# One-core GNN stack: bits and f columns by transfers, norm statistics on GpSimd, wider softmax products

## The chip, the cores and the metric

The kernel runs on one core of one Trainium2 chip. The metric is the device time of one execution in microseconds. The time before the change is the median of three runs.

## The reference, cut to what matters

Each of 64 independent graphs has 256 nodes with 256 features, and goes through four layers. Each layer's result is added to its input and normalised over the features.

```python
# layer 0: transformer layer with 8 heads of 32, masked by the symmetric adjacency
allowed = (adj > 0) | (swapaxes(adj, 1, 2) > 0) | eye
attn = softmax(where(allowed, (q * scale) @ k.T, -inf))          # per head
x = layernorm(x + (attn @ v) @ Wo.T + bo) ; x = layernorm(x + relu(x @ W1.T + b1) @ W2.T + b2)
# layers 1 and 2: graph attention
h = x @ W ; f = h @ a[0] ; g = h @ a[1]
e = leaky_relu(f[:, None] + g[None, :], 0.2), masked by adj > 0
out = softmax(e) @ h            # (+ bias in layer 1, elu in layer 2)
# layer 3: two relational convolutions with elu, on masks adj == 1
# after each layer: x = _layernorm(x + layer(x))
def _layernorm(x, eps=1e-5):
    m = mean(x) ; v = var(x)
    return (x - m) / sqrt(v + eps)
```

## The kernel before

A graph's work is written as a list of operations with estimated costs and lags, their reads and writes, and rings of buffers. A planner inside the kernel (`Plan.schedule`) runs through all 64 graphs' operations once, when the kernel is built, and fixes the order of the instructions on each engine; several graphs are under way at once, and on the chip every engine goes through its list strictly in that order. `pe(...)`, `dve(...)` and `act(...)` put an operation on TensorE, VectorE and ScalarE; `op("POOL", ...)` and `op("SP", ...)` on GpSimd and SyncE. The marks "uses" and "waits" tell the planner to keep GpSimd's norm operations apart from VectorE operations with two SBUF operands; they are no waits on the chip.

The helpers that the change touches or that the prediction speaks of (bodies cut where nothing changes):

```python
def add_later(xt, yt, reads):
    op("POOL", 0.6, lambda: nc.gpsimd.dma_start(xt(), yt(), accum_op=ALU.add), [xt, *reads], [xt], lag=3.0)

def bounced(xt):            # a transposed copy: blocks on VectorE, then rows through DRAM
    dve(0.63, ... nc.vector.transpose(turned..., xt...), [xt], [turned], "uses")
    for a in range(4):
        op("SP", 0.5, lambda a=a: nc.sync.dma_start(rows()...[:, :, a, :], turned()[32 * a : 32 * a + 32]...), [turned], [(rows, a)], lag=SENT)
    op("SP", 0.5, lambda: nc.sync.dma_start(xT()..., rows()...), [rows], [xT], lag=BACK)

def layer_norm(y):
    mv, stat = new("mv", [P, NB, 2]), new("st", [P, NB, 6])
    rstd = new("rstd", [P, 2, NB])
    def stats():
        for i in range(NB):
            nc.vector.bn_stats(stat()[:, i, :], y()[:, i, :])
        for i in range(NB):
            nc.vector.bn_aggr(mv()[:, i, :], stat()[:, i, :])
    def root():
        nc.gpsimd.tensor_scalar(rstd()[:, 0, :], mv()[:, :, 1], 1.0, EPS, op0=ALU.mult, op1=ALU.add)
        nc.gpsimd.tensor_tensor(rstd()[:, 0, :], rstd()[:, 0, :], neghalf[:, 0:NB], op=ALU.pow)
        nc.gpsimd.tensor_tensor(rstd()[:, 1, :], mv()[:, :, 0], rstd()[:, 0, :], op=ALU.mult)
        nc.gpsimd.tensor_scalar(rstd()[:, 1, :], rstd()[:, 1, :], -1.0, 1.0, op0=ALU.mult, op1=ALU.mult)
    def apply():
        for i in range(NB):
            nc.scalar.activation(y()[:, i, :], y()[:, i, :], AF.Identity, bias=rstd()[:, 1, i : i + 1],
                                 scale=rstd()[:, 0, i : i + 1])
    dve(0.88, stats, [y], [mv, stat])
    op("POOL", 1.6, root, [mv], [rstd], port="waits", lag=0.4)
    act(1.0, apply, [y, rstd], [y])

def masks(adj):
    bits, am, gm = tok("bits", BF16), tok("am", BF16), tok("gm", BF16)
    pt = new("bank", [P, NB, N], BF16)
    dve(0.33, lambda: nc.vector.tensor_scalar(bits(), adj(), 0.0, None, op0=ALU.is_gt), [adj], [bits], "uses")
    def issue():
        for i in range(NB):
            for j in range(NB):
                nc.tensor.transpose(pt()[:, i, j * P : (j + 1) * P], bits()[:, j, i * P : (i + 1) * P], ident_b)
    pe("full", 0.22, issue, [bits], [pt], [am, gm])
    dve(0.33, lambda: nc.vector.tensor_scalar(gm(), pt(), BIG, NO_EDGE, op0=ALU.mult, op1=ALU.add), [pt], [gm])
    dve(0.33, lambda: nc.vector.tensor_tensor(am(), pt(), bits(), op=ALU.max), [pt, bits], [am])
    ...                      # the diagonal of am is set

def attention(xT, am):
    ...                      # projections; two halves kt of the keys
        pe("row", 0.97, scores, [qk], s, [p[kt, r] for r in range(4)])
        for r in range(4):
            pr, k = p[kt, r], 8 * g + 4 * kt + r
            act(0.58, lambda pr=pr, k=k, sr=s[r]: nc.scalar.activation(
                pr(), sr(), AF.Exp, accum_out=seen_sum[:, k : k + 1]), [s[r]], [pr])
            dve(0.60, lambda pr=pr, kt=kt: nc.vector.tensor_tensor(
                pr(), pr(), am()[:, kt, None, :].to_broadcast([P, KB, N]), op=ALU.mult), [pr, am], [pr], "uses")
    both = [new("both", [P, KB, N]) for r in range(4)]
    for r in range(4):
        dve(0.60, lambda r=r: nc.vector.tensor_tensor(both[r](), p[0, r](), p[1, r](), op=ALU.add),
            [p[0, r], p[1, r]], [both[r]], "uses")
    ...                      # products with v, reciprocals

def feed_forward(x1, xt):
    add_row_later(xt, ln2b)
    x1T = transposed(x1)
    with_row(x1, ln1g, ALU.mult)
    with_row(x1, b2, ALU.add)
    ...

def gat(xt, layer, gm, seen, bias, finish):
    xT, xT_at = bounced(xt)
    ...                      # h = x W, with the columns f and g beside it
    pf = new("bank", [P, N])
    def spread():
        for i in range(NB):
            nc.tensor.transpose(pf()[:, i * P : (i + 1) * P],
                                h()[:, i, F_COL : F_COL + 1].to_broadcast([P, P]), ident)
    pe("full", 0.22, spread, [(h, 0), (h, 1)], [pf], [e])
    for i in range(NB):
        dve(0.40, lambda i=i: nc.vector.scalar_tensor_tensor(e()[:, i, :], pf(), h()[:, i, G_COL : G_COL + 1],
                                                             gm()[:, i, :], op0=ALU.add, op1=ALU.min),
            [pf, (h, i), gm], [(e, i)])
    dve(0.60, lambda: nc.vector.scalar_tensor_tensor(e(), e(), SLOPE, e(), op0=ALU.mult, op1=ALU.max), [e], [e],
        "uses")
    act(0.52, lambda: nc.scalar.activation(e(), e(), AF.Exp), [e], [e])
    ...                      # products e h, each row divided by its sum

# one graph
xT = input_transposed()
adj = load("adj", adj_graph[g], I32)
am, gm = masks(adj)
xt = load("x", x_graph[g], F32)
add_row_later(xt, bo, [c_bo])
ctxT = attention(xT, am)
x1 = product_plus(lambda c: ctxT()[:, c, :], [ctxT, c_wo], lambda c: wo[:, c, :], KB, xt)
layer_norm(x1)
xt = feed_forward(x1, load("xr", x_graph[g], F32))
xt = layer1(xt, gm)
xt = layer2(xt, gm)
rel = relation(load("adj", adj_graph[g], I32))
rdeg = new("rdeg", [P, NB])
h = conv(conv(xt, 0, rel, rdeg), 1, rel, rdeg)
add(h, xt)
layer_norm(h)
op("SP", 0.4, lambda: nc.sync.dma_start(out_graph[g], h()), [h], [])
```

## Time and profile before

| | before |
|---|---|
| time, median of 3 | 2897.77 us (2897.14 to 2898.14) |
| span of the profiled execution | 2897.1 us, 50588 instructions |
| TensorE clock granted | 0.991 of full, mean |
| HBM | 157.43 MB read, 83.89 MB written |
| transfers issued by SyncE | 37.7% of 16 DMA engines' span |
| transfers issued by GpSimd | 8.5% |
| `rows<-turned`, `T<-rows`, `blocks<-in_x` | 1024, 256 and 512 transfers |

The profile names engines PE (TensorE matmuls), PEld (its weight loads, which overlap matmuls), DVE (VectorE), ACT (ScalarE), POOL (GpSimd) and SPq (the queue of SyncE, which issues transfers). A group line gives the line of the kernel, the engine, the operation, output and input tiles with their shapes, and the count; then busy us and the mean ns of one; then the idle time of the engine just before instructions of the group, and what ended it. Line numbers can be those of a helper: L657 is the matmul of every product. An f32 matmul appears as two instructions.

The page's chain of work that ended last is TensorE for 82% of the span, with 67% on line L657 alone; VectorE has 10%, ScalarE 3%, transfers 2%.

### The profile page before, as it was taken

The page shows a single profiled execution, that of the slowest core. Times are in us where ns is not written, and L with a number is a line of the kernel's source. Part 1 is how long each engine was busy: PE and PEld are TensorE (multiplying, and loading weights), DVE is VectorE, ACT ScalarE, POOL GpSimd, SP SyncE. Part 2 cuts the span into 40 slices and gives each one's busy share as a digit, 9 for nine tenths or more (in the row PEclk, how much of TensorE's full clock was granted, in tenths as well). Part 3 has the DMA queues.
Part 4 walks back from the last instruction along what each step waited for, and adds up shares of the span by engine and source line. Part 5 has one row for each costly group of instructions (what it writes and reads, how often), then busy time and mean ns, then how long its engine had stood idle before and what let it go on. Part 6 is the DMA issues. An engine that isn't in the chain of part 4 may idle for free.

```text
span 2897.1 us, 50588 instructions
## 1 busy us (share of the span) xinstructions
PE 2805.3 (97%) x16182; PEld 2128.1 (73%) x16182; DVE 2523.0 (87%) x6557; ACT 1540.4 (53%) x3713; POOL 789.1 (27%) x1685
## 2 busy tenths in 40 slices
PE   8999999999999999999999999999999999999975
PEld 6776777777777767777777777777777777777853
DVE  6879899989989898999889898899888998999686
ACT  3555555546455555655555465555555655555343
POOL 2232223222223222222222322232231332222221
PEclk9999999999999999999999999999999999999998
DMA  7454455445444444454444544444444544443342
GB/s 183 81 108 88 99 101 102 89 101 102 95 92 100 87 94 94 98 101 93 104 97 93 98 99 99 100 91 102 86 93 96 109 88 93 105 90 72 67 83 70
DMA packets 844512, 278.32 MB, mean 96 GB/s; under 512 B 692656, under 2 KB 810672, under 8 KB 844240
## 3 DMA queue, kind: packets, MB, share of 16 engines
q1 hardware_dynamic: 808800, 240.27, 37.7%
q0 software_dynamic: 35440, 34.76, 8.5%
q8 instruction: 131, 2.15, 0.3%
q14 instruction: 141, 1.16, 0.1%
HBM read 157.43 MB, written 83.89 MB: 83 GB/s over the span
## 4 chain that ended last, share of the span: by engine, by line
PE 82%; DVE 10%; ACT 3%; DMA 2%; issue 2%; POOL 1%; SPq 1%; DVEq 0%; POOLq 0%; ACTq 0%
PE bank L657 67%; PE bank L919 4%; PE bank L776 3%; PE bank L751 3%; PE bank L771 2%; DMA rows<-turned 2%; DVE p L759 1%; PE bank L618 1%; DVE turned L629 1%; PE bank L839 1%; SPq L633 1%; DVE st L666 1%; DVE o L929 1%; DVE both L763 1%; DVE e L844 1%
## 5 line engine op out<-in xcount | busy, mean ns | idle before, releaser
L671 POOL TENSOR_SCALAR rstd<-mv 128x2 f32<-128x2 f32 x384 | 104.4, 272 | 1869.8 <-DVE mv L668 1496.7
L678 ACT ACTIVATE X<-X,rstd 128x256 f32<-128x256 f32 x640 | 349.8, 597 | 244.7 <-POOL rstd L674 230.1
L657 PE MATMUL bank<-cw,T 128*128 128x512 f32 x1024 | 467.9, 600 | 9.6 <-DMA T<-rows 9.1
L657 PE MATMUL bank<-T,w 128*128 128x256 f32 x2048 | 471.6, 380 | 5.2 <-ACT p L757 2.6
L657 PE MATMUL bank<-w,hid 128*128 128x256 f32 x2048 | 460.1, 380 | 0.0
L657 PEld LDWEIGHTS bank<-w,hid 128*128 128x128 f32 x2048 | 385.9, 190 | 62.7 <-issue 10.4
L657 PEld LDWEIGHTS bank<-T,w 128*128 128x128 f32 x2048 | 382.7, 190 | 64.5 <-issue 6.9
L757 ACT ACTIVATE p<-bank 128x512 f32<-128x512 f32 x512 | 299.9, 598 | 87.8 <-PE bank L751 87.6
L657 PEld LDWEIGHTS bank<-cw,T 128*128 128x128 f32 x1024 | 192.2, 192 | 209.3 <-issue 195.2
L759 DVE TENSOR_TENSOR p<-p,am 128x512 f32<-128x512 f32 x512 | 332.8, 680 | 10.8 <-ACT p L757 10.7
L672 POOL TENSOR_TENSOR rstd<-rstd,neghalf 128x2 f32<-128x2 f32 x384 | 305.7, 796 | 32.1
L809 ACT ACTIVATE hid<-bank,col_b 128x256 f32<-128x256 f32 x512 | 209.4, 474 | 113.8 <-PE bank L657 112.1
L657 PE MATMUL bank<-xT,wqkv 128*128 128x256 f32 x1024 | 251.6, 387 | 13.4 <-DVE xT L650 12.9
L657 PE MATMUL bank<-h,e 128*128 128x259 f32 x1024 | 253.8, 388 | 11.0 <-ACT e L849 9.3
L657 PE MATMUL bank<-gw,T 128*128 128x258 f32 x1024 | 249.1, 384 | 2.1 <-ACT inv L783 1.5
L657 PEld LDWEIGHTS bank<-h,e 128*128 128x128 f32 x1024 | 192.7, 192 | 66.6 <-issue 19.3
L666 DVE BATCH_NORM_STATS2 st<-X 128x6 f32<-128x256 f32 x640 | 237.5, 413 | 1.8
L906 ACT CAST hi<-bank 128x256 fp32r<-128x256 f32 x256 | 94.6, 370 | 263.4 <-PE bank L657 262.6
L657 PEld LDWEIGHTS bank<-xT,wqkv 128*128 128x128 f32 x1024 | 189.7, 192 | 54.0 <-issue 13.5
L780 DVE RECIPROCAL inv<-bank 128x256 f32<-128x256 f32 x128 | 220.0, 1734 | 8.8 <-PE bank L776 8.6
L657 PEld LDWEIGHTS bank<-gw,T 128*128 128x128 f32 x1024 | 191.1, 191 | 36.7 <-issue 5.2
L629 DVE STREAM_TRANSPOSE turned<-X 128x512 f32<-128x512 f32 x192 | 134.9, 703 | 45.0 <-DMA rows<-turned 23.0
(121 smaller groups left out, 4775.4 us busy)
## 6 DMA issues: line engine op xcount, KB each, us to landing
rows<-turned SPq DMA_DIRECT2D x1024, 64.0 KB, 2.2
T<-rows SPq DMA_DIRECT2D x256, 256.0 KB, 2.8
adj<-in_adj_dram SPq DMA_DIRECT2D x128, 256.0 KB, 3.0
blocks<-in_x_dram SPq DMA_DIRECT2D x512, 32.0 KB, 2.3
x<-in_x_dram SPq DMA_DIRECT2D x64, 256.0 KB, 3.0
xr<-in_x_dram SPq DMA_DIRECT2D x64, 256.0 KB, 2.8
xr<-row_ln_b POOLq DMA_DIRECT2D x64, 256.0 KB, 4.4
x<-row_bo POOLq DMA_DIRECT2D x64, 256.0 KB, 4.8
```

What stands on the lines that cost most here:

```text
L629: dve(0.63, lambda: nc.vector.transpose(turned().rearrange("p b q n -> p (b q n)"), xt().rearrange("p i (k b c) -> p b (i k) c", k=KB, b=4 ...
L657: nc.tensor.matmul(dst, lhsT=lhs(c), rhs=rhs(c), start=(c == 0), stop=(c == n - 1))
L666: nc.vector.bn_stats(stat()[:, i, :], y()[:, i, :])
L671: nc.gpsimd.tensor_scalar(rstd()[:, 0, :], mv()[:, :, 1], 1.0, EPS, op0=ALU.mult, op1=ALU.add)
L672: nc.gpsimd.tensor_tensor(rstd()[:, 0, :], rstd()[:, 0, :], neghalf[:, 0:NB], op=ALU.pow)
L678: nc.scalar.activation(y()[:, i, :], y()[:, i, :], AF.Identity, bias=rstd()[:, 1, i : i + 1], scale=rstd()[:, 0, i : i + 1])
L757: act(0.58, lambda pr=pr, k=k, sr=s[r]: nc.scalar.activation(pr(), sr(), AF.Exp, accum_out=seen_sum[:, k : k + 1]), [s[r]], [pr])
L759: dve(0.60, lambda pr=pr, kt=kt: nc.vector.tensor_tensor(pr(), pr(), am()[:, kt, None, :].to_broadcast([P, KB, N]), op=ALU.mult), [pr, am] ...
L780: dve(1.62, lambda hg=hg, pc=pc: nc.vector.reciprocal(inv()[:, hg, :], pc()[:, 1, :]), [pc], [(inv, hg)])
L809: act(0.36, lambda f=f, k=k, ph=ph: nc.scalar.activation(hid()[:, f + k, :], ph()[:, k, :], AF.Relu, bias=b1[:, f + k : f + k + 1]), [ph, ...
L906: act(0.27, lambda i=i, po=po: nc.scalar.copy(hi()[:, i, 0:D], po()[:, D:]), [po], [(hi, i)])
L919: nc.tensor.matmul(pa()[:, 0:n], lhsT=rel()[:, i, j * P : (j + 1) * P], rhs=part()[:, i, 0:n], start=(c == 0), stop=(c == len(terms) - 1))
```

## The change: what it does and what it is for

Seven things change.

1. The adjacency bits (bf16) are transposed by four transposing transfers for each graph (128x128 each, SBUF to SBUF) in place of four TensorE transposes into PSUM. The masks `gm` and `am` are then made from SBUF.
2. The column f, which each partition needs as a row, is spread by transfers in place of two TensorE transposes with a broadcast operand: VectorE turns 32x32 blocks of the column repeated 32 times, two transfers write them as rows to DRAM, and one transfer reads these rows into all 128 partitions. `e` is made from SBUF.
3. The norm's two halves of statistics, which VectorE's `bn_stats` leaves, are joined on GpSimd in place of VectorE's `bn_aggr`; GpSimd then has nine small operations for a norm in place of four.
4. The row b2 is added by an accumulating transfer, in place of VectorE.
5. The last residual is added by an accumulating transfer, except in the last two graphs.
6. The softmax products and sums on VectorE take 1024 elements at a time in place of 512. The buffers double in size and halve in number.
7. The planner is told a spacing of 44 in place of 46 us between graphs.

Its aim is to take work off TensorE and VectorE and give it to the DMA engines and GpSimd.

The diff, with unchanged lines cut and the indentation shortened:

```diff
@@ ... @@
-RINGS = {"x": 3, "adj": 4, "bits": 2, "am": 2, "gm": 6, "T": 4, "qk": 2, "v": 2, "p": 12, "both": 4, "inv": 1, "ctxT": 2, "X": 8,
-         "xr": 1, "hid": 1, "h": 3, "e": 3, "n": 1, "rel": 3, "hi": 2, "lo": 2, "o": 4, "blocks": 1, "turned": 1, "xT": 2}
-DRAM = {"rows": 6}
+RINGS = {"x": 3, "adj": 4, "bits": 2, "am": 2, "gm": 6, "T": 4, "qk": 2, "v": 2, "p": 6, "both": 2, "inv": 1, "ctxT": 2, "X": 8,
+         "xr": 1, "hid": 1, "h": 3, "e": 3, "n": 1, "rel": 3, "hi": 2, "lo": 2, "o": 4, "blocks": 1, "bitsT": 1, "f": 2, "own": 2, "turned": 1, "xT": 2}
+DRAM = {"f_row": 2, "rows": 6}
@@ ... @@
-    PERIOD = 46.0
+    PERIOD = 44.0
@@ ... @@
 def layer_norm(y):
-    mv, stat = new("mv", [P, NB, 2]), new("st", [P, NB, 6])
-    rstd = new("rstd", [P, 2, NB])
+    stat, t, rstd = new("st", [P, NB, 2, 3]), new("mv", [P, NB, 4]), new("rstd", [P, 2, NB])
         for i in range(NB):
-            nc.vector.bn_stats(stat()[:, i, :], y()[:, i, :])
-        for i in range(NB):
-            nc.vector.bn_aggr(mv()[:, i, :], stat()[:, i, :])
+            nc.vector.bn_stats(stat()[:, i].rearrange("p h k -> p (h k)"), y()[:, i, :])
-        nc.gpsimd.tensor_scalar(rstd()[:, 0, :], mv()[:, :, 1], 1.0, EPS, op0=ALU.mult, op1=ALU.add)
-        nc.gpsimd.tensor_tensor(rstd()[:, 0, :], rstd()[:, 0, :], neghalf[:, 0:NB], op=ALU.pow)
-        nc.gpsimd.tensor_tensor(rstd()[:, 1, :], mv()[:, :, 0], rstd()[:, 0, :], op=ALU.mult)
-        nc.gpsimd.tensor_scalar(rstd()[:, 1, :], rstd()[:, 1, :], -1.0, 1.0, op0=ALU.mult, op1=ALU.mult)
+        tensor_tensor, tensor_scalar = nc.gpsimd.tensor_tensor, nc.gpsimd.tensor_scalar
+        m, s, d = t()[:, :, 0], t()[:, :, 1], t()[:, :, 2]
+        scale, shift = rstd()[:, 0, :], rstd()[:, 1, :]
+        tensor_tensor(t()[:, :, 0:2], stat()[:, :, 0, 1:3], stat()[:, :, 1, 1:3], op=ALU.add)
+        tensor_tensor(d, stat()[:, :, 0, 1], stat()[:, :, 1, 1], op=ALU.subtract)
+        tensor_tensor(d, d, d, op=ALU.mult)
+        tensor_scalar(s, s, 4 / D, 4 * EPS, op0=ALU.mult, op1=ALU.add)
+        tensor_tensor(d, d, s, op=ALU.add)
+        tensor_tensor(d, d, neghalf[:, 0:NB], op=ALU.pow)
+        tensor_tensor(shift, m, d, op=ALU.mult)
+        tensor_scalar(shift, shift, -1.0, 1.0, op0=ALU.mult, op1=ALU.mult)
+        tensor_scalar(scale, d, 2.0, 1.0, op0=ALU.mult, op1=ALU.mult)
         for i in range(NB):
-    dve(0.88, stats, [y], [mv, stat])
-    op("POOL", 1.6, root, [mv], [rstd], port="waits", lag=0.4)
+    dve(0.56, stats, [y], [stat])
+    op("POOL", 2.5, root, [stat], [t, rstd], port="waits", lag=0.6)
 def masks(adj):
-    pt = new("bank", [P, NB, N], BF16)
+    pt = tok("bitsT", BF16)
-    def issue():
-        for i in range(NB):
-            for j in range(NB):
-                nc.tensor.transpose(pt()[:, i, j * P : (j + 1) * P], bits()[:, j, i * P : (i + 1) * P], ident_b)
-    pe("full", 0.22, issue, [bits], [pt], [am, gm])
-    dve(0.33, lambda: nc.vector.tensor_scalar(gm(), pt(), BIG, NO_EDGE, op0=ALU.mult, op1=ALU.add), [pt], [gm])
-    dve(0.33, lambda: nc.vector.tensor_tensor(am(), pt(), bits(), op=ALU.max), [pt, bits], [am])
+    for i in range(NB):
+        for j in range(NB):
+            op("SP", 1.3, lambda i=i, j=j: nc.sync.dma_start_transpose(
+                pt()[:, i, j * P : (j + 1) * P], bits()[:, j, i * P : (i + 1) * P]), [bits], [(pt, 2 * i + j)], lag=3.5)
+    dve(0.25, lambda: nc.vector.tensor_scalar(gm(), pt(), BIG, NO_EDGE, op0=ALU.mult, op1=ALU.add), [pt], [gm], "uses")
+    dve(0.33, lambda: nc.vector.tensor_tensor(am(), pt(), bits(), op=ALU.max), [pt, bits], [am], "uses")
@@ ... @@
+def heads(t):
+    return t().rearrange("p r k n -> p (r k) n")
 def attention(xT, am):
@@ ... @@
-        for r in range(4):
-            p[kt, r] = new("p", [P, KB, N])
+        for r in (0, 2):
+            p[kt, r] = new("p", [P, 2, KB, N])
         def scores(kt=kt, s=s):
@@ ... @@
-        pe("row", 0.97, scores, [qk], s, [p[kt, r] for r in range(4)])
+        pe("row", 0.97, scores, [qk], s, [p[kt, 0], p[kt, 2]])
-            pr, k = p[kt, r], 8 * g + 4 * kt + r
-            act(0.58, lambda pr=pr, k=k, sr=s[r]: nc.scalar.activation(
-                pr(), sr(), AF.Exp, accum_out=seen_sum[:, k : k + 1]), [s[r]], [pr])
-            dve(0.60, lambda pr=pr, kt=kt: nc.vector.tensor_tensor(
-                pr(), pr(), am()[:, kt, None, :].to_broadcast([P, KB, N]), op=ALU.mult), [pr, am], [pr], "uses")
-    both = [new("both", [P, KB, N]) for r in range(4)]
-    for r in range(4):
-        dve(0.60, lambda r=r: nc.vector.tensor_tensor(both[r](), p[0, r](), p[1, r](), op=ALU.add),
+            pr, j, k = p[kt, r - r % 2], r % 2, 8 * g + 4 * kt + r
+            act(0.58, lambda pr=pr, j=j, k=k, sr=s[r]: nc.scalar.activation(
+                pr()[:, j], sr(), AF.Exp, accum_out=seen_sum[:, k : k + 1]), [s[r]], [(pr, j)])
+            if j == 1:
+                dve(1.14, lambda pr=pr, kt=kt: nc.vector.tensor_tensor(
+                    heads(pr), heads(pr), am()[:, kt, None, :].to_broadcast([P, 2 * KB, N]), op=ALU.mult),
+                    [pr, am], [pr], "uses")
+    both = {}
+    for r in (0, 2):
+        both[r] = new("both", [P, 2, KB, N])
+        dve(1.14, lambda r=r: nc.vector.tensor_tensor(heads(both[r]), heads(p[0, r]), heads(p[1, r]), op=ALU.add),
@@ ... @@
         def values(hg=hg, pc=pc):
-                nc.tensor.matmul(pc()[32 * r : 32 * r + 32, 1, :], lhsT=ones, rhs=both[r]()[:, hg, :],
+                nc.tensor.matmul(pc()[32 * r : 32 * r + 32, 1, :], lhsT=ones, rhs=both[r - r % 2]()[:, r % 2, hg, :],
-                                     rhs=p[kt, r]()[:, hg, :], start=(kt == 0), stop=(kt == NB - 1))
-        pe("col", 1.32, values, [v] + both + list(p.values()), [pc], [ctxT, inv])
+                                     rhs=p[kt, r - r % 2]()[:, r % 2, hg, :], start=(kt == 0), stop=(kt == NB - 1))
+        pe("col", 1.32, values, [v, *both.values(), *p.values()], [pc], [ctxT, inv])
@@ ... @@
-    with_row(x1, b2, ALU.add)
+    add_row_later(x1, b2)
@@ ... @@
-    pf = new("bank", [P, N])
-    def spread():
+    own, rows, pf = new("own", [P, NB * 32]), new("f_row", [32, N]), new("f", [P, N])
+    def turn():
         for i in range(NB):
-            nc.tensor.transpose(pf()[:, i * P : (i + 1) * P],
-                                h()[:, i, F_COL : F_COL + 1].to_broadcast([P, P]), ident)
-    pe("full", 0.22, spread, [(h, 0), (h, 1)], [pf], [e])
+            nc.vector.transpose(own()[:, i * 32 : (i + 1) * 32], h()[:, i, F_COL : F_COL + 1].to_broadcast([P, 32]))
+    dve(0.22, turn, [(h, 0), (h, 1)], [own], "uses")
+    for i in range(NB):
+        op("SP", 0.51, lambda i=i: nc.sync.dma_start(rows()[:, i * P : (i + 1) * P].rearrange("r (b n) -> b r n", b=4),
+                                                     own()[:, i * 32 : (i + 1) * 32]), [own], [(rows, i)], lag=2.2)
+    op("SP", 0.54, lambda: nc.sync.dma_start(pf(), rows()[None, :, :].to_broadcast([4, 32, N])), [rows], [pf], lag=4.3)
     for i in range(NB):
-            [pf, (h, i), gm], [(e, i)])
+            [pf, (h, i), gm], [(e, i)], "uses")
@@ ... @@
-add(h, xt)
+if g < B - 2:
+    add_later(h, xt, [xt])
+else:
+    add(h, xt)
```

## The prediction

> **What bounds the kernel now.** I read the busy shares first, then the busy time by stretch, then the order of time on TensorE around the instructions that go, then groups and transfers.
>
> The engine line of the page and the busy times of three stretches (start, steady run, end; columns: us of the stretch, then busy us of each engine with its instructions, granted clock, transfer share, GB/s):
>
> ```profile
> PE 2805.3 (97%) x16182; PEld 2128.1 (73%) x16182; DVE 2523.0 (87%) x6557; ACT 1540.4 (53%) x3713; POOL 789.1 (27%) x1685
> ...
> 0.00:40.00 40.00, 25.99 (x169) 20.75 (x170) 18.74 (x43) 9.01 (x24) 14.29 (x24) 0.88 0.83 203
> 100.00:2700.00 2600.00, 2570.24 (x15041) 1955.43 (x15035) 2325.29 (x6016) 1426.73 (x3459) 723.61 (x1536) 1.00 0.47 95
> 2733.00:2898.00 165.00, 116.11 (x419) 74.20 (x417) 117.95 (x369) 62.16 (x127) 30.68 (x83) 0.90 0.36 76
> ```
>
> In the steady run PE is idle for 2600 - 2570.2 = 29.8 us only (1.1%). PE idles at the start (14.0 us of the first 40) and in the last 165 us (48.9 us), where the last graphs' chains are alone: together 93 us, which is the span less PE's busy time. So TensorE's queue of work sets the time, and DVE, at 89% of the steady run, follows. In the steady run a shorter VectorE list pays only through those 29.8 us; a shorter TensorE list pays in full.
>
> What the removed TensorE work costs. First the two groups, then the order of time (start, us, engine, line, tiles):
>
> ```profile
> L839 PE MATMUL bank<-ident,h 128*128 128x128 f32 x256 | 52.1, 279 | 8.9 <-DVE h L830 4.5 <-ACT h L828 4.0 <-ACT p L757 0.2
> ...
> L695 PE MATMUL bank<-ident_b,bits 128*128 128x128 bf16 x256 | 24.9, 219 | 0.4 <-ACT h L828 0.4
> ```
>
> ```profile
> 2715.77 0.38 PE L839 MATMUL bank<-ident,h 128*128 128x128 f32 x2
> 2715.99 1.91 PE L657 MATMUL bank<-gw,T 128*128 128x258 f32 x8
> ...
> 97.38 0.39 PE L695 MATMUL bank<-ident_b,bits 128*128 128x128 bf16 x4
> 97.60 1.95 PE L657 MATMUL bank<-wqkv,xT 128*128 128x256 f32 x8
> ```
>
> The groups claim 52.1 + 24.9 = 77.0 us. But a pair of f transposes begins at 2715.77 and the next matmul at 2715.99; four bit transposes begin at 97.38 and the next matmul at 97.60. Each set holds the queue for 0.22 us; the rest of its "busy" 0.38 lies under the next matmul. The group times therefore count overlap twice, and I use 0.22 us.
>
> **What the Trainium skill says.** "Perfetto Trace Analysis", section Identifying the Most-Contended Engine: matmul busy share is a poor measure of distance to the limit because matmuls are pipelined. The trace agrees (0.38 against 0.22 above); I use the spacing and the idle time. "DMA: Bandwidth & Descriptors", section on why a DMA increments its semaphore by 16: the number of DMA engines must divide the slowest dimension of both sides, so one whose outer dimension is 4 uses at most four. The broadcast of f has a leading 4, and so has the destination of the row write; no transfer of the kernel before is of this shape. "SBUF — State Buffer", section Who interferes with whom: a VectorE operation with two SBUF inputs and a GpSimd operation that reads SBUF block each other for a whole instruction. The trace agrees in that GpSimd's first norm operation has a median of 193 ns, a mean of 272 and a longest of 1197. "VectorE: DVE Perf Modes", tier table: a two-byte scalar operation wholly in SBUF may run at four elements a cycle, with a PSUM operand at two at most; gm reads PSUM today and takes 414 ns for 512.
>
> **The change, part by part.** There are 64 graphs, with 6 norms and 2 graph attention layers (each with one f) in each.
>
> TensorE loses 64 x 0.22 = 14.1 us for the bits and 128 x 0.22 = 28.2 us for f: 42 us. With the f pairs go the waits before them, 8.9 us in the group line; a later instruction inherits some, so I count 6. Nothing is added to TensorE. Three of a graph's PSUM tiles go too; what TensorE waits for PSUM lies within the 29.8 us.
>
> VectorE, from these groups:
>
> ```profile
> L668 DVE BATCH_NORM_AGGREGATE mv<-st 128x2 f32<-128x6 f32 x768 | 115.5, 174 | 1.0
> ...
> L598 DVE TENSOR_TENSOR X<-X,row_b 128x512 f32<-128x512 f32 x64 | 43.7, 682 | 0.1
> L609 DVE TENSOR_TENSOR o<-o,X 128x512 f32<-128x512 f32 x64 | 43.6, 682 | 0.2
> ```
>
> Aggregation -115.5; row addition -43.7; last residual -43.6 x 62/64 = -42.2. Wider operations: 512 elements take 684 ns and 256 take 414, so 1024 take about 684 + 2 x 270 = 1224 ns: 256 x 1.22 = 312 against 332.8 for the mask products, 128 x 1.22 = 156 against 167.5 for the sums, -32 in all. gm at perhaps 280 ns, as long as a 256-element two-byte product takes (281): 64 x 0.13 = -9. The e operation reads f from SBUF, 471 to perhaps 414 ns: -15. Added are 256 small transposes: the 512-element one takes 703 ns[...], so about 0.2 us each: +50. Net -207: VectorE falls from 2523 to about 2316 us, 81% of the new span. This lies beside TensorE.
>
> GpSimd: a norm takes 1.61 us of four operations (272 + 796 + 268 + 275 ns); nine take 1.61 + 5 x 0.27 = 2.97. Added 384 x 1.36 = 522, and 126 more accumulating transfers at 1.27 us of issue = 160: 789 becomes about 1471 us, half the span, still free. Latency of one norm: five steps of 0.28 more, two aggregations of 0.15 less: +1.1 us.
>
> Transfers to landing, today (KB, us):
>
> ```profile
> rows<-turned SPq DMA_DIRECT2D x1024, 64.0 KB, 2.2
> T<-rows SPq DMA_DIRECT2D x256, 256.0 KB, 2.8
> ...
> x<-row_bo POOLq DMA_DIRECT2D x64, 256.0 KB, 4.8
> ```
>
> f today reaches VectorE 0.64 us after its transposes begin. Afterwards: two small transposes 0.35, a second issue 0.6, one trip of 2.2, and a trip of 128 KB on few engines, which I take as 4 us: about 7.2, so +6.5 us per layer, +13 per graph. The bits gain some 8 us, but loaded early. SyncE issues 43 transfers per graph in place of 33. At 0.63 us for each row write, 0.34 for a T read and 0.4 to 0.45 for loads its issue time is about 17 of 45 us per graph; ten more add 6 to 8, or some 55%.
>
> What of this reaches the end: in the steady run a graph's longer latency is filled by other graphs; I add 3 us. In the tail the last graph goes through two layers and five norms: 13 + 5.5 = 18.5 us longer; other graphs fill about half, +9. At the start the first mask comes by transfer before the first softmax product: +3. Sum: 2897.8 - 42 - 6 + 3 + 9 + 3 = 2865.
>
> **Rivals.** (1) A transfer on the path takes the place of TensorE's transposes. SyncE and VectorE work strictly in order, so a late f stops VectorE before e, and a late row write stops the next T read. For it: SyncE's queue already waits 272.8 us, 298 times, for row writes in front of the T reads. Against it: in the steady run TensorE waits for a T read once, 0.3 us; the planned order leaves slack. It would give 0.3 to 1 us per graph, 2885 to 2930. (2) VectorE was the real limit, since TensorE's few steady waits are mostly for ScalarE and VectorE; then 207 us less there empties the 29.8 us and shortens the tail, where VectorE is busy 71%: 2820 to 2840. Against it is that those waits are only 1.1%. (3) GpSimd's doubled load blocks VectorE on the shared port, and the longer 1.2 us products block GpSimd: norm latencies double and VectorE wins little, 2870 to 2890. (4) The transposing transfers are much slower than plain ones and clog the queue before the T reads: over 2950; nothing in this trace speaks to it.
>
> **Range and chances.** The 42 us are the firm part. Around them stand the tail (0 to +20), the waits of the steady run (-20 to +40) and the start (0 to +6). I take 2825 to 2910. Faster by over 2% means below 2839.8: 16 us more than the slots and recovered waits minus any losses, so nearly all losses must vanish and rival 2 hold in part: 0.20. Slower by over 2% needs rival 4 or a severe form of rival 1: 0.07. Within 2%: 0.73.
>
> **What would show it.** Right: TensorE's busy time down by 40 to 50 us and not 77; its idle time in the steady run between 20 and 45 us; VectorE near 2316 us and GpSimd near 1470; f landing about 4 us after issue; about 10 us more in the last stretch. Wrong: PE below 97% of the steady run with waits that name f, T or bitsT (rivals 1, 4); small GpSimd operations well above a mean of 272 ns, or two-input VectorE operations stretched beyond 1.22 us (rival 3); steady idle near zero and a shorter tail (rival 2).

## The result, and the profile after

| | before | after |
|---|---|---|
| time, median | 2897.77 us | 3071.47 us (3065.95 to 3077.4) |
| ratio to before | 1 | 1.06, 95% interval 1.0576 to 1.0624 |
| span of the profiled execution | 2897.1 us | 3066.0 us, 51242 instructions |
| TensorE clock granted, mean | 0.991 | 0.978 |
| HBM read, written | 157.43, 83.89 MB | 174.21, 88.08 MB |
| SyncE's, GpSimd's transfers, share of 16 DMA engines | 37.7%, 8.5% | 40.3%, 15.0% |

The change costs 174 us. The prediction was 2865, so it missed by 206 us and had the wrong sign.

The engine line of the page of the changed kernel:

```profile
PE 2829.9 (92%) x15670; PEld 2111.3 (69%) x15670; DVE 2376.5 (78%) x5535; ACT 1531.3 (50%) x3713; POOL 1462.8 (48%) x3731
```

TensorE has 512 instructions fewer and is busy 24.6 us longer. It is idle for 3066.0 - 2829.9 = 236.1 us, where it was 91.8 before. The two differences, 24.6 + 144.3, make up the 168.9 us between the two profiled spans.

Busy times by stretch of the changed kernel (start, steady run, last 166 us; columns as in the prediction):

```profile
0.00:40.00 40.00, 23.44 (x155) 19.71 (x156) 17.51 (x34) 9.01 (x24) 12.88 (x23) 0.88 0.81 201
100.00:2700.00 2600.00, 2444.56 (x13706) 1829.04 (x13698) 2059.40 (x4772) 1333.22 (x3250) 1284.82 (x3227) 0.99 0.57 112
2900.00:3066.00 166.00, 111.25 (x364) 68.98 (x362) 110.11 (x325) 60.12 (x122) 50.83 (x174) 0.84 0.42 88
```

The loss is in the middle line. In the same 2600 us TensorE executed 13706 instructions instead of 15041, and was idle for 155.4 us instead of 29.8. To place it in time I took the moments at which the two traces have done the same number of matmuls, leaving out the transposes that were removed. The changed kernel is 14 us late at the 1000th, 41 at the 4000th, 67 at the 7500th, 104 at the 11000th, 149 at the 14000th, 154 at the 15000th and 169 at the end. So the start costs about 14 us, the steady run about 140, and the tail about 15. This measure is rough, because the two orders differ and the n-th matmul is mostly not the same one: a kernel with the work of the kernel before in another order (the last run below) is up to 22 us late on the way and 1 us at the end.

What the engines waited for. From the list of all engines' waits, before (columns: us in total, times, longest us):

```profile
ACT X L678 <- POOL rstd L674: 230.1, 125, 9.6
```

From the same view after:

```profile
ACT X L685 <- POOL rstd L681: 436.9, 217, 12.6
POOL o L603 <- DVE o L951: 291.8, 38, 23.6
...
DVE e L860 <- DMA f<-f_row: 130.0, 69, 5.9
```

ScalarE waits almost twice as long for GpSimd's last norm operation as before. GpSimd waits 291.8 us to issue the transfer of the last residual, a wait that the kernel before did not have. VectorE waits for f, also new. TensorE's own waits after:

```profile
PE bank L657 <- ACT e L865: 66.0, 42, 5.3
PE bank L657 <- DMA T<-rows: 32.1, 20, 9.1
PE bank L935 <- DVE hi L928: 29.9, 18, 4.5
PE bank L935 <- DVE lo L923: 20.5, 20, 2.5
```

Before, these four were 9.3, 9.8, 9.4 and 7.0 us. No single operand holds TensorE up. Many of its inputs come late, which I read as whole graphs being behind their places in the order.

GpSimd's groups after (the power, then the first and second operation of a norm; columns as in the prediction):

```profile
L678 POOL TENSOR_TENSOR mv<-mv,neghalf 128x2 f32<-128x2 f32 x384 | 307.5, 801 | 30.0
L673 POOL TENSOR_TENSOR mv<-st 128x4 f32<-128x4 f32 x384 | 150.3, 392 | 826.1 <-DVE st L665 706.1 <-DVE r L870 76.6 <-DVE rdeg L941 23.7
L674 POOL TENSOR_TENSOR mv<-st 128x2 f32<-128x2 f32 x384 | 142.8, 372 | 0.0
```

The nine means of a norm add up to 392 + 372 + 263 + 267 + 291 + 801 + 313 + 295 + 287 = 3281 ns. The planner was told 2.5 us. It was also told 0.6 us for the issue of an accumulating transfer, as in the kernel before; in the trace it takes 1.28 us in the median, and 0.94 us for the residual's. Hence GpSimd's real list is longer than the list that was planned, and each of its operations comes later than its place among the other engines assumed.

A piece of the order of time of the changed kernel shows how GpSimd stands in its own way (start, us, engine, line, tiles; in brackets the idle time before it):

```profile
1514.67 0.75 DVE L665 BATCH_NORM_STATS2 st<-X 128x6 f32<-128x256 f32 x2
...
1515.93 0.69 DVE L951 SCALAR_TENSOR_TENSOR o<-e,o 128x512 f32<-128x512 f32 x1
...
1516.92 0.89 POOL L603 DMA_DIRECT2D o<-X  x1 [8.37 <-DVE seen_fg L844]
...
1517.51 0.53 POOL L673 TENSOR_TENSOR mv<-st 128x4 f32<-128x4 f32 x1
```

The statistics of a norm were ready at 1514.67 + 0.75 = 1515.42. GpSimd was idle, but next in its list stood the residual's transfer, whose `o` was finished at 1516.62. (The bracket names `seen_fg`, another VectorE operation that ended just as the transfer was issued.) The transfer was issued, and only then, 2.1 us after its operand, did the norm begin. An engine with 52% of its time free made ready work wait.

### The profile page after: what moved, and what is told of

It reads as the page before. It is cut to its first block, busy times and chain, and to the rows that moved or that the text cites. A ratio compares the mean times of both kernels' runs of the same rounds, so it can differ in the third digit from the quotient of the medians.

```text
span 3066.0 us, 51242 instructions
## 1 busy us (share of the span) xinstructions
PE 2829.9 (92%) x15670; PEld 2111.3 (69%) x15670; DVE 2376.5 (78%) x5535; ACT 1531.3 (50%) x3713; POOL 1462.8 (48%) x3731
## 3 DMA queue, kind: packets, MB, share of 16 engines
q1 hardware_dynamic: 900448, 269.66, 40.3%
HBM read 174.21 MB, written 88.08 MB: 86 GB/s over the span
## 5 line engine op out<-in xcount | busy, mean ns | idle before, releaser
L685 ACT ACTIVATE X<-X,rstd 128x256 f32<-128x256 f32 x640 | 349.2, 594 | 438.1 <-POOL rstd L681 436.9
L673 POOL TENSOR_TENSOR mv<-st 128x4 f32<-128x4 f32 x384 | 150.3, 392 | 826.1 <-DVE st L665 706.1
L657 PE MATMUL bank<-cw,T 128*128 128x512 f32 x1024 | 476.4, 609 | 15.5 <-DMA T<-rows 12.1
L768 DVE TENSOR_TENSOR p<-p,am 128x1024 f32<-128x1024 f32 x256 | 307.1, 1214 | 35.2 <-ACT p L765 34.4
L657 PE MATMUL bank<-h,e 128*128 128x259 f32 x1024 | 266.0, 403 | 66.4 <-ACT e L865 66.0
L678 POOL TENSOR_TENSOR mv<-mv,neghalf 128x2 f32<-128x2 f32 x384 | 307.5, 801 | 30.0
L603 POOL DMA_DIRECT2D o<-X x62 | 59.3, 956 | 382.9 <-DVE o L951 291.8
```

The costliest lines, as they stand in the source:

```text
L657: nc.tensor.matmul(dst, lhsT=lhs(c), rhs=rhs(c), start=(c == 0), stop=(c == n - 1))
L673: tensor_tensor(t()[:, :, 0:2], stat()[:, :, 0, 1:3], stat()[:, :, 1, 1:3], op=ALU.add)
L678: tensor_tensor(d, d, neghalf[:, 0:NB], op=ALU.pow)
L768: dve(1.14, lambda pr=pr, kt=kt: nc.vector.tensor_tensor(heads(pr), heads(pr), am()[:, kt, None, :].to_broadcast([P, 2 * KB, N]), op=ALU.m ...
```

## The experiments

In the quoted expectations G stands for the theory that GpSimd's part costs the time, and P for its cause being the planner's too short figures. The rival reasons are the trip of f, the transposing transfers of the bits, the wider products, the spacing of 44, and a mere change of order.

### Each part undone in the changed kernel

Four kernels, each the changed kernel with one part of the change put back. Joining the statistics on VectorE again:

```diff
-tensor_tensor(t()[:, :, 0:2], stat()[:, :, 0, 1:3], stat()[:, :, 1, 1:3], op=ALU.add)   # and eight more
+nc.vector.bn_aggr(mv()[:, i, :], stat()[:, i, :])                                     # and four GpSimd operations
-op("POOL", 2.5, root, [stat], [t, rstd], port="waits", lag=0.6)
+op("POOL", 1.6, root, [mv], [rstd], port="waits", lag=0.4)
```

> The changed kernel with the norm's statistics joined on VectorE again and four GpSimd operations for a norm (all else as changed). Theory G: ScalarE's waits for GpSimd fall from 437 to near the 230 us of before, TensorE's waits for normed rows vanish, time falls by 60 to 120 us, to 2950 to 3010. Theory F: the f waits stay near 130 us, VectorE gets 115 us of work back, time within 3030 to 3080. Theory S: no change, as SyncE's list is the same.

Measured: 2993.52 us, ratio 1.033 (1.0291 to 1.0369), 78 us less than the changed kernel.

Both accumulating transfers undone:

```diff
-add_row_later(x1, b2)
+with_row(x1, b2, ALU.add)
-add_later(h, xt, [xt])      # for all but the last two graphs
+add(h, xt)
```

> The changed kernel with the row b2 and the last residual added on VectorE again (all else as changed); GpSimd's queue no longer stands before the residual's transfer (292 us waiting for o in the changed kernel), with norm operations of other graphs behind it. Theory G in the form that this standing is what delays the norms: time falls by 60 to 120 us, to 2950 to 3010. Theory F: 3040 to 3080. Theory S: no change.

Measured: 3000.45 us, ratio 1.0354 (1.0301 to 1.0406), 71 us less. The time is as G forecast, the reason is not: ScalarE waits for the norms almost as long as in the changed kernel (426.8 us, against 436.9).

```profile
ACT X L685 <- POOL rstd L681: 426.8, 215, 12.1
```

With the statistics undone, on the other hand, GpSimd's wait for `o` rose from 291.8 to 343.8 us while the time fell by 78. So the transfers cost time, but that they do it by delaying the norms is not shown, and GpSimd's wait for `o` does not measure it.

f by TensorE again:

```diff
-dve(0.22, turn, [(h, 0), (h, 1)], [own], "uses")       # and its three transfers
+pe("full", 0.22, spread, [(h, 0), (h, 1)], [pf], [e])
```

> The changed kernel with f spread by TensorE again (all else as changed). Theory F, the trip of f sets the time: VectorE no longer stands 130 us before e (69 waits in the changed kernel), TensorE no longer 66 us before the products with e; the time falls by 110 to 170 us, to 2900 to 2960, though TensorE gets 28 us of work back. Theory G, GpSimd's queue sets it: norms stay late (ScalarE waits 437 us for them) and the time falls by under 60 us, to 3010 or more. Theory S, SyncE's load as a whole: 384 of 2790 issues and 215 us of 1803 us of issue time go, about a third of what the change added (596 us), so about a third of the 174 us: 3010.

Measured: 3039.37 us, ratio 1.0488 (1.0458 to 1.0519), 32 us less.

The bits by TensorE again:

```diff
-op("SP", 1.3, ... nc.sync.dma_start_transpose(...), [bits], [(pt, 2 * i + j)], lag=3.5)    # four
+pe("full", 0.22, issue, [bits], [pt], [am, gm])
```

> The changed kernel with the bits transposed by TensorE again (all else as changed). SyncE loses 256 issues of 1.22 us, 313 of the 596 us that the change added to its issue time. Theory S: f and the row writes leave sooner, f waits fall to under half, time falls by about 90 us, to 2980. Theory F in its narrow form (f's own trip, not the queue): f waits stay near 130 us, time 3050 to 3090. Theory G: no change.

Measured: 3041.73 us, ratio 1.0496 (1.0466 to 1.0527), 30 us less. None of the three forecasts holds.

The two GpSimd parts are the largest, and each of these four makes the changed kernel slower.

### Both GpSimd parts undone, one of them alone, wide products alone, true figures

The changed kernel without its two GpSimd parts (both edits above):

> The changed kernel with all of GpSimd's new work undone: statistics joined on VectorE, row b2 and last residual added on VectorE; bits and f still go by transfers, softmax operations still wide. Theory G (GpSimd's in-order queue is the larger part; what undoing each half gave, 78 and 71 us, adds up): 2910 to 2935. Rival C (each undoing only frees the same slack, any relief helps alike): about 2975 to 2995, no better than one alone. Rival F (f and bits keep a floor of their own, 32 + 30 us): 2940 to 2965.

Measured: 2929.72 us, ratio 1.0108 (1.0086 to 1.013). That is 142 us less, close to 78 + 71. The parts add up, and they are 82% of the 174 us.

The kernel before with only the norm's statistics moved to GpSimd, with the figure of the change (2.5 us):

```diff
-dve(0.88, stats, [y], [mv, stat])
-op("POOL", 1.6, root, [mv], [rstd], port="waits", lag=0.4)
+dve(0.56, stats, [y], [stat])
+op("POOL", 2.5, root, [stat], [t, rstd], port="waits", lag=0.6)    # with the nine operations
```

> The kernel before with one part of the change alone: the norm's statistics joined on GpSimd (nine operations). Theory G in the form that the longer norm itself hurts: 50 to 80 us slower, 2950 to 2980. Rival Q (it hurts only where the accumulating transfers stand in the same queue, as in the changed kernel): within 15 us of before, 2885 to 2915, since VectorE gets 115 us of work less and the planner is told most of the longer norm.

Measured: 2972.81 us, ratio 1.0247 (1.0196 to 1.0298), 74 us more than before.

The kernel before with only the 1024-element products and sums:

```diff
-"p": 12, "both": 4
+"p": 6, "both": 2          # each of twice the size
-dve(0.60, ... pr(), pr(), am()[:, kt, None, :].to_broadcast([P, KB, N]) ...)
+dve(1.14, ... heads(pr), heads(pr), am()[:, kt, None, :].to_broadcast([P, 2 * KB, N]) ...)
```

> The kernel before with one part of the change alone: softmax products and sums of 1024 elements in half as many, twice as large buffers. The undone parts of the changed kernel add up to 211 us against 174 us in all, so this part and the spacing would be worth up to -37 us: 2860 to 2890. Rival: the wider products wait for two softmax operations of ScalarE (34 us in the changed kernel) and hold buffers longer: 2900 to 2920.

Measured: 2905.79 us, ratio 1.0021 (1.0013 to 1.0028). The saving on VectorE brings nothing.

The changed kernel, with all its work as it is, but with the planner told nearly what the trace shows:

```diff
-op("POOL", 0.6, lambda: nc.gpsimd.dma_start(xt(), yt(), accum_op=ALU.add), [xt, *reads], [xt], lag=3.0)
+op("POOL", 1.3, lambda: nc.gpsimd.dma_start(xt(), yt(), accum_op=ALU.add), [xt, *reads], [xt], lag=3.5)
-op("POOL", 2.5, root, [stat], [t, rstd], port="waits", lag=0.6)
+op("POOL", 3.3, root, [stat], [t, rstd], port="waits", lag=0.6)
```

> The changed kernel with the same work and only the planner's figures for GpSimd set to what the trace of the changed kernel shows: 3.3 us for a norm's operations in place of 2.5, 1.3 us for the issue of an accumulating transfer in place of 0.6, landing 3.5 us after it in place of 3.0. Theory P (the order was planned on too short GpSimd times, so engines stand in order behind late norms): 50 to 110 us faster than the changed kernel, 2960 to 3020. Rival L (the load and latency themselves cost the time, whatever the order): 3050 to 3080.

Measured: 2967.28 us, ratio 1.0228 (1.0178 to 1.0278), 104 us less than the changed kernel with not one operation fewer. The three figures were changed together, so their shares are not told apart here. Its waits, in the view of all engines:

```profile
ACT X L685 <- POOL rstd L681: 271.2, 136, 12.2
...
POOL o L603 <- DVE o L951: 182.0, 33, 19.2
```

Against 436.9 and 291.8 us: the norms are late less often.

### The same figure in the kernel with statistics alone

```diff
-op("POOL", 2.5, root, [stat], [t, rstd], port="waits", lag=0.6)
+op("POOL", 3.3, root, [stat], [t, rstd], port="waits", lag=0.6)
```

> The kernel before with the norm's statistics joined on GpSimd, as in the run of that part alone (74 us slower), but with the planner told 3.3 us for GpSimd's part in place of 2.5. Theory P (the wrong figure costs the time): at least two thirds of the 74 us come back, 2890 to 2920, and ScalarE's waits for GpSimd fall from 454 us to about 300. Rival L (nine operations and the longer norm cost it): 2950 to 2975.

Measured: 2906.13 us, ratio 1.0028 (1.0021 to 1.0036). One number in the plan is worth 67 of the 74 us. ScalarE's waits with the figure 2.5:

```profile
ACT X L685 <- POOL rstd L681: 365.0, 210, 9.4
...
ACT o L685 <- POOL rstd L681: 89.1, 41, 5.6
```

and with 3.3:

```profile
ACT X L685 <- POOL rstd L681: 234.8, 120, 9.3
```

The kernel before has 230.1 us in this wait. A new order alone moved the time by at most 18 us in two trials (below), so 67 us are hardly the luck of an order. The cause of the statistics' cost is therefore not the work on GpSimd, whose busy time in the steady run is about the same in both (1183 us with 2.5, 1201 with 3.3), but where the plan put it. The steady run with 2.5, then with 3.3 (the fifth engine is POOL):

```profile
100.00:2700.00 2600.00, 2532.02 (x14620) 1909.35 (x14623) 2207.32 (x5182) 1389.43 (x3365) 1183.28 (x3203) 1.00 0.46 94
```

```profile
100.00:2700.00 2600.00, 2562.80 (x14963) 1945.12 (x14962) 2251.17 (x5270) 1414.15 (x3438) 1200.74 (x3283) 1.00 0.46 95
```

The pair also shows that VectorE was not a bound: with 2455.7 us instead of 2523.0 of VectorE the kernel is no faster than before.

### f, and the bits

The corrected plan once more, with the landing of f told 3 us later:

```diff
-op("SP", 0.54, lambda: nc.sync.dma_start(pf(), rows()...), [rows], [pf], lag=4.3)
+op("SP", 0.54, lambda: nc.sync.dma_start(pf(), rows()...), [rows], [pf], lag=7.3)
```

> The changed kernel with true GpSimd figures in the plan (2967 us) and, in addition, 3 us more told for the landing of f (7.3 in place of 4.3), so that e is planned later and VectorE stands less in front of it. Theory P for f: VectorE's waits for f fall from 94 to under 40 us, the time falls by 15 to 45 us, to 2920 to 2950. Rival L for f (the longer chain costs it through buffers and graphs under way): 2960 to 2990.

Measured: 2964.68 us, ratio 1.0218 (1.0158 to 1.0278), the same as the corrected plan. Yet VectorE's waits show what the edit did; with 4.3 us:

```profile
DVE e L860 <- DMA f<-f_row: 93.9, 66, 4.5
```

and with 7.3 us:

```profile
DVE e L860 <- DMA f<-f_row: 12.0, 7, 3.9
```

So 82 us of VectorE standing in front of f were free, to within what an order alone moves: what the eye falls on in the waits was not what cost time.

The kernel before with f by transfers alone (the edit of the third experiment, turned round):

> The kernel before with one part alone: f spread by transfers. Theory F: VectorE waits 50 to 130 us for f and the time rises by 20 to 50 us in spite of TensorE's 28 us less, 2915 to 2950. Rival: f's lateness in the changed kernel came from what the late norms push back; alone it is on time, f waits under 40 us, 2865 to 2890.

Measured: 2946.69 us, ratio 1.0156 (1.0126 to 1.0185): 48 us slower, though 28 us of TensorE's slots are gone. TensorE's longest wait is then

```profile
PE bank L656 <- ACT e L853: 35.5, 18, 7.3
```

against this before:

```profile
PE bank L657 <- ACT e L849: 9.3, 8, 2.2
```

The trip itself, in the changed kernel, for one graph:

```profile
1516.54 0.30 DVE L852 STREAM_TRANSPOSE own<-h 128x32 f32<-128x32 f32 x2
...
1516.77 1.19 SPq L856 DMA_DIRECT2D f_row<-own  x2
...
1521.65 0.56 SPq L858 DMA_DIRECT2D f<-f_row  x1
...
1527.11 0.88 DVE L860 SCALAR_TENSOR_TENSOR e<-f,h,gm 128x256 f32<-128x256 f32 x2 [1.38 <-DMA f<-f_row]
```

From the end of the small transposes (1516.84) to e it is 10.3 us, and over all 128 trips the median is 10.7. In the kernel before, e began 0.68 us after the first of TensorE's two transposes began (median of 128).

The same with f's three transfers issued by ScalarE's queue in place of SyncE's, since SyncE's issue time had risen from 42% of the span to 59% in the changed kernel, and to 49% with f alone:

```diff
-op("SP", 0.51, ... nc.sync.dma_start(...)) ; op("SP", 0.54, ... nc.sync.dma_start(...))
+op("ACT", 0.6, ... nc.scalar.dma_start(...)) ; op("ACT", 0.6, ... nc.scalar.dma_start(...))
```

> The kernel before with f spread by transfers, as in the run of that part alone (2947 us), but its three transfers issued by ScalarE's queue in place of SyncE's. Theory S (f waits 4.5 us at the median for its turn among SyncE's row writes, of 9.7 us from the small transposes to e): the trip falls to about 8 us and the time by 15 to 35 us, to 2912 to 2932. Rival L (the trip's own length, and ScalarE's queue is as much in order as SyncE's): 2940 to 2965.

Measured: 2951.2 us, ratio 1.0172 (1.0129 to 1.0216). VectorE's wait for f fell from 61.7 to 17.7 us, and the time did not move. Taking f off SyncE's queue does not bring its cost back. The trip itself hardly changed, though: the second issue came 1.2 us sooner, but e followed the small transposes after 9.5 us in place of 9.7 (medians), where about 8 was forecast. So a truly shorter trip was not tried.

The kernel before with the bits by transfers alone (the edit of the fourth experiment, turned round):

> The kernel before with one part alone: the bits transposed by transfers. TensorE loses 64 x 0.22 = 14 us; bits are loaded early, so if nothing else moves 2880 to 2890. Theory S (SyncE's queue: 313 us of issue more, in front of row writes and T reads): 2905 to 2935, with TensorE's waits for T reads well above the 9.8 us of before.

Measured: 2919.82 us, ratio 1.0067 (1.0044 to 1.009), 21 us slower. The time lies in the range of theory S, but its sign is missing: TensorE waits 9.6 us for T reads, and the row writes and T reads land in 2.2 and 2.7 us, as before. VectorE waits 12.5 us in all for `bitsT`, 9.5 of them before the first `am`, and the kernel is 12 us late already at the 1000th matmul. That suggested that the start alone is to blame. So I left the first two graphs' bits on TensorE:

```diff
+if g < 2:    # transposed by TensorE, as before
+else:        # transposed by transfers
```

> The kernel before with the bits by transfers from the third graph on; the first two graphs keep TensorE's transposes. With bits by transfers from the start, 12 of its 21 us of loss were there by the 1000th matmul. Theory start (the transfers stand in front of first loads and masks): 2905 to 2912. Rival (the start has other causes, or the loss only moves on): 2915 to 2925.

Measured: 2936.9 us, ratio 1.0123 (1.0083 to 1.0164), 38 us slower. VectorE's wait before the first `am` is gone, and the kernel is 6 us late at the 1000th matmul, but 44 at the 11000th: the start was mended and more was lost later. Both forecasts were too low, and the theory of the start falls. It falls also for f and the bits together, in the changed kernel without its GpSimd parts, with both kept on TensorE in the first two and the last five graphs:

> The changed kernel with GpSimd's new work undone (2930 us) and f and bits by transfers only from the third to the sixth graph before the last; the first two and last five graphs use TensorE. By its matmuls' progress that kernel lost 17 us against before by the 1000th matmul and 11 more after the 15000th, and nothing between. Theory start and tail: 2895 to 2908. Rival (the losses move to where the transfers begin): 2920 to 2935.

Measured: 2939.4 us, ratio 1.0132 (1.0095 to 1.0168), against 2929.72 with all graphs by transfers, and again above both forecasts.

### Order alone

The spacing of 44 in the kernel before:

```diff
-    PERIOD = 46.0
+    PERIOD = 44.0
```

> The kernel before with only the planner's spacing of graphs at 44 in place of 46, the last part of the change alone; it also shows how far a new order without any new work moves the time. Expected 2880 to 2915; theory P says an order from right figures moves little, so within 15 us of before.

Measured: 2897.36 us, ratio 0.9994 (0.9987 to 1.0001): nothing. At 14952 of 15670 places of TensorE's list (without the transposes) stands a matmul of the same tiles as before, so this is hardly a new order.

Last, how much does a new order cost by itself? Two kernels with exactly the work of the kernel before and one figure of the plan moved a little; both get a new order, with the same tiles at 3373 and 4109 of the 15670 places.

```diff
-pe("full", 0.22, issue, [bits], [pt], [am, gm])
+pe("full", 0.20, issue, [bits], [pt], [am, gm])
```

> The kernel before with exactly its work and one planner figure changed a little: 0.20 in place of 0.22 us for the four bit transposes, which gives a wholly new order on all engines. Theory O (the order of before is a picked one; any new order costs 10 to 40 us, and that is what bits by transfers, 21 to 38 us, and part of f are): 2908 to 2940. Rival W (new orders are worth the same, the losses come with the added transfers): 2890 to 2905.

Measured: 2916.89 us, ratio 1.0064 (1.0044 to 1.0084), 18 us slower.

```diff
-SENT, BACK = 3.0, 4.5
+SENT, BACK = 3.1, 4.5
```

> The kernel before with exactly its work and one other planner figure changed: 3.1 in place of 3.0 us for the landing of the row writes, again a wholly new order. Theory O: 2908 to 2940. Rival W: 2890 to 2905. Both new orders together also say how far single runs of this study can be told apart.

Measured: 2897.68 us, ratio 0.9994 (0.9984 to 1.0004).

So a new order of unchanged work may cost nothing or 0.6%. The 21 us of the bits are hardly more than that; the 38 us of the run with two graphs left out are. I cannot say how much of either the bits themselves cost. I can only say that their 14 us of slots were not collected.

### The account of the 174 us

Wrong figures for GpSimd: 3071.5 - 2967.3 = 104 us. What remains of the two GpSimd parts with better figures: 2967.3 - 2929.7 = 38. f, bits, wide products and spacing together: 2929.7 - 2897.8 = 32. Each of these is good to some 18 us, by which an order alone moved the time. The last 32 cannot be divided further: alone, the parts cost 48, 21, 7 and 0 us, which is 76, each with an order of its own.

## Why the prediction was wrong, and where it was right

**The step that failed** is "in the steady run a graph's longer latency is filled by other graphs; I add 3 us". With the slots and recovered waits, the prediction's steady run was 42 + 6 - 3 = 45 us shorter. It became 140 us longer, and this gap of 185 us is nearly the whole miss of 206. The order is fixed when the kernel is built, and no engine can take up another graph that happens to be ready. A norm of about 3.2 us that was planned at 3.3 cost 7 us; planned at 2.5 it cost 74. So latency that the plan knows may be filled, and latency that it was told too short is passed on. Telling it f's longer trip, however, gained nothing. I had the proof before me: I worked out 2.97 us for a norm from the profile, and the diff told the planner 2.5.

**"GpSimd becomes about 1471 us, half the span, still free"** had the right number (1462.8) and the wrong word. The number was partly luck: the norm measured 3.28 us for my 2.97, and GpSimd's groups add up to some 1590 us, of which about 128 lie under one another, which I had not counted. What mattered was how late an operation in its in-order list was, and the busy share does not tell that. The residual's transfer, which I counted as 1.27 us of issue, held the list up by its wait (291.8 us in all), though that wait does not measure its cost.

**Rivals.** Rival 1 had the right mechanism, an in-order queue standing before a late operand, but I placed it at f and the row writes on SyncE and VectorE. VectorE's standing before f was free, and the real place was GpSimd. That its upper end, 2930, is what the kernel without the GpSimd parts took (2929.7) is no confirmation, since the wide products and a new order are in that figure too. Rival 2 is false: VectorE's list became 146 us shorter and nothing came back. Rival 4 is false as far as the landing times show it: with the bits alone, `bitsT` lands in 2.4 us, the row writes in 2.2.

Rival 3 is half right, and its mechanism is where the planner's figure went wrong. VectorE's products are not stretched (1214 ns), but GpSimd's operations are. The first one of a norm (shortest, median and longest, in ns):

```profile
L673 POOL TENSOR_TENSOR mv<-st x384: 194/202/4500, 42.4 to 3058.2; 128x4 f32<-128x4 f32 x192
```

Its mean is 392. The nine medians of a norm add up to 2.28 us, the nine means to 3.28: the plan's 2.5 us fits operations that nothing disturbs. The whole difference, 383 us, lies in 664 of the 3456 operations, those that took over 1.3 times their median. VectorE was inside an operation with two SBUF operands for 84% of their time, for 9% of the others' time, and for 36% of the span. This stretching costs little by itself: with statistics alone and 3.3 us in the plan it is nearly as large (345 us), and that kernel is only 7 us slower than before. So it cost time mainly through the plan, which rival 3's 2870 to 2890 did not foresee.

**Sums.** That 2839.8 needs "16 us more than the slots and recovered waits" is wrong: 2897.8 - 48 - 2839.8 is 10 us; 16 is the distance from the slots alone. SyncE's added issue time, which I put at 6 to 8 us per graph, was 596 / 64 = 9.3, since a transposing transfer takes 1.22 us to issue.

**TensorE.** I called the 42 us "the firm part". The slots are gone, but busy time rose by 24.6 us, so 67 us of busy time came from elsewhere. The granted clock explains a part. In the steady run the trace has 17 pieces at half clock with 64.8 us together, before 2 with 6.8. At half speed, (64.8 - 6.8) / 2 = 29 us of work time are lost at most. Over the whole span the pieces rise from 10 to 29, from 52.7 to 136.4 us, at most 42 us. The pieces follow idle gaps (last section), so the clock adds to what the gaps cost. The other 25 or so us of busy time I have not accounted for.

**VectorE** fell by 146.5 us, not by 207. The aggregation is the main error: I subtracted its group time of 115.5 us, but with the statistics alone moved, VectorE's busy time fell by 2523.0 - 2455.7 = 67.3. Small operations overlap the one before them, just as TensorE's transposes do, and I applied this correction to one engine only. The e operation makes up most of the rest: 476 ns with f in SBUF, not 414.

**Right:** the wide products (1214 ns for 1224), the small transposes (188 ns for 200), gm (292 ns for 280), and f's landing, 4.4 us in the median from issue to e where e waited, for "4 us". Too short was the way to the second issue of f: a median of 5.4 us from the transposes' end. By the rough count above the start cost about 14 us, not 3, and the tail about 15, not 9; both signs were right.

**What stays open.** Why f's trip costs 48 us alone. VectorE's standing and SyncE's queue do not explain it. What is left is its length: a graph that takes 10 us more in each of two layers holds its buffers longer, so fewer graphs are ready to fill TensorE's list. This is argued, not shown. The test would be more buffers for h and e; it was not tried. Part of the 48 us may be the new order. Open too are the way in which the accumulating transfers cost their 71 us, and what the remaining 38 us of the GpSimd parts consist of.

## What to carry to other kernels

Where the order of instructions is planned on cost figures, work that moves to another engine must enter the plan with the durations and issue times of a trace, and with means under load, not with what an undisturbed operation takes (2.28 us here, in place of 3.28); one figure that was 0.8 us short cost 67 us. Before calling an engine free by its busy share, look at what stands in its list in front of the operations that others wait for, and at how late those are. And when TensorE is 99% busy, do not add latency to each graph's chain to save 1.5% of its slots, unless the order can be shown to fill it; compare the gain also with what a new order of the same work does, here 0.6%.

## What the runs showed of the hardware that was not expected

An idle gap well under 3.4 us can be followed by a slower TensorE clock. The Trainium skill, "TensorE: Matmul & The Clock Gate", section Part 1: The HAM clock gate, says that the clock falls to half after an idle window of about 3.4 us and returns after as much busy time. The trace agrees in the size of the pieces: they are 3.4 us or multiples of it. It does not agree that a gap of 3.4 us is needed. In the 6.8 us ahead of each of the 17 pieces of the steady run, TensorE's longest gap was 3.4 to 4.3 us in four cases, and 0.9 to 2.8 us in the other thirteen (ends of matmuls are modelled, so these are good to a few tenths). The page's later remark, under A second HAM failure mode, that frequent small idle times make the clock swing does not fit well either: in 13 of the 17 cases the 6.8 us held a single gap. Nor is a short gap enough. A piece began within 6.9 us of the start of 4 of the 38 gaps of 1 to 2 us, of 8 of the 13 gaps of 2 to 3 us, and of all four gaps of over 3.4 us. The 17 pieces all begin on one grid of 3.41 us. TensorE's gaps of over 0.1 us rose from 45 to 152 in the steady run, those of over 1 us from 11 to 56.

A transposing transfer of 128x128 bf16 within SBUF took 1.22 us to issue (median of 256). In the kernel with the bits alone, the row writes and T reads landed in 2.2 and 2.7 us, against 2.2 and 2.8 before. Where an operation of three operands (256 f32) read f from SBUF instead of PSUM, it took 476 ns instead of 471.
